# A decoder's last feed-forward layer: hidden units in seven blocks of 128 tokens in place of eight batches of 112

## The chip, the core and the metric

The kernel runs on one core of one Trainium2 chip. The metric is the device time of one execution in microseconds (us), as the median of several runs. The core has five engines with a queue each: TensorE (PE in the profile, its weight loads PEld), VectorE (DVE), ScalarE (ACT), GpSimd (POOL) and SyncE (SP), which here only issues transfers. Every queue is worked off in order, so an instruction that waits holds up all that stand behind it on its engine.

## What is computed

The reference is a decoder of four layers on `x`, 8 batches of 112 tokens with 256 features. Each layer adds an attention, a cross attention and a feed-forward part (FFN) to `x`. The change touches the last part, the FFN of layer 3, alone:

```
def nvfp4_linear(x, w, s_in):
    s_w = fp4_global_scale(w)
    xq = fake_quant_nvfp4(x, s_in)      # blocks of 16: one rounded scale, values rounded to 8 levels
    wq = fake_quant_nvfp4(w, s_w)
    return jnp.einsum('bsh,oh->bso', xq, wq)
gate_out = nvfp4_linear(x, gate_w, s_in[0])
up_out = nvfp4_linear(x, up_w, s_in[0])
hidden = jax.nn.silu(gate_out) * up_out                 # 1024 features for each token
return nvfp4_linear(hidden, down_w, s_in_down[0])
```

Its input is the normalised `x` (256 features), its result is added to `x`, and the sum is the kernel's output. Rounding acts on each token by itself, so the tokens can be cut into groups in any way.

## The kernel before

The kernel builds its program with a library that puts in the waits between engines, and that also chooses the order of instructions on each engine: among those that it takes to be ready it prefers the one that stands earlier in the program's text. Inside a `manual_schedule` block the order on PE, DVE and ACT is that of the text. A tile that is asked for under a name with one buffer (`bufs=1`) is the same memory each time, and the new use waits for the last reader of the old one.

`l3_ffn` (lines 2378 to 2485) holds the last FFN. Its weights are rounded and turned earlier (`l3_weights`, in the background of the layer 2 FFN) and lie in `self.wq`, 16 bits wide.

*Input.* The tokens come in two halves of four batches. For each half the kernel takes mean and variance of `x` (`stats`, lines 439 to 465), writes the normalised values `xn` (line 2403), their magnitudes `mag` with ACT (2410), rounds them (`quantise`), turns the rounded `xq` with eight transposes on PE (2416) and copies the turned values to `xqT` with ACT (2421). This lies outside the block with the order by hand.

*Rounding.* `quantise` is a generator: it writes instructions to DVE alone, and gives control back to its caller at each `yield`. In the order of its steps:

```
step 0   block_max: pairwise maxima of mag, 16 to 1, four instructions (L2261)
step 1   scales of the blocks, nine small instructions (L2289 to L2302)
step 2   qa = src * z                    (L2306, 32 bits)
step 3   high half | 1                   (L2309)
step 4   clip; exponent; its bound       (L2311, L2313, L2314, 16 bits)
step 5   add, subtract                   (L2316, L2317)
step 6   dst = b * scale, 1024 columns   (L2322); one more such step when n is 2048
```

*Hidden units.* `hidden(b0)` makes the 1024 hidden features of two batches, in four units of 512 columns: four matrix products on PE into `gu` (gate and up, two banks, two buffers), ACT's Silu (`sg`, 2436), DVE's product (`hid`, 2437), which frees `gu`, and ACT's magnitude (`mag`, 2440). It too is a generator, with a `yield` after each unit. Its tiles have 112 of 128 partitions in use, a token in each.

*The rounds.* The block with the order by hand runs the four units of batches 0 and 1, and then four rounds over pairs of batches. A round is `quantise` over the pair's 2 x 1024 columns, and between its steps stand: at step 2 the adds (2459) and output transfers (2460, on SP) of the pair before; at steps 2 to 5 the four units of the next pair; at steps 6 and 7 `turned` (eight transposes of one batch's rounded `hq` on PE, 2448, and one ACT copy of 896 columns into `hqT`, 2450) and `result` (eight products with the down weights into `y`, 428). In the last round `turned` of the last batch copies with DVE, and the two results and adds come after the round.

All matrix products are recorded under line 428, the helper `mm`.

Of the kernel before, what the change touches and what calls it, by code (L numbers as in the profile page):

```python
# [23 lines left out]
BF16 = mybir.dt.bfloat16  # L24
I16 = mybir.dt.int16
AF = mybir.ActivationFunctionType
ALU = mybir.AluOpType
# [4 lines left out]
P = 128  # L32
S, NB, D = 112, 8, 256
T = S * NB
HT = T // 2
HB = NB // 2
# [299 lines left out]
def drain(steps):  # L336

    while True:
        try:
            next(steps)  # L340
        except StopIteration as stop:
            return stop.value
# [31 lines left out]
class _Kernel:  # L374
# [2004 lines left out]
    def l3_ffn(self):  # L2379
        nc, tc = self.nc, self.tc  # L2380
        g, u = (m.rearrange("p (k n) -> p k n", k=2) for m in self.wq[:2])
        d = self.wq[2].rearrange("p (k n) -> p k n", k=8)
        with ExitStack() as ctx:
            acts = ctx.enter_context(tc.tile_pool(name="l3f", bufs=1))
            pool = ctx.enter_context(tc.tile_pool(name="l3f_x", bufs=1))
            work = ctx.enter_context(tc.tile_pool(name="l3f_h", bufs=2))
            ps = ctx.enter_context(tc.tile_pool(name="ps_l3f", bufs=2, space=PSUM))
            s_in, s_down = self.v("l3f_s_in"), self.v("l3f_s_in_down")

            sc = self.t(acts, [P, 3], "sc")  # L2390
            inv = self.t(acts, [P, 2], "inv")
            nc.vector.reciprocal(inv[:, 0:1], s_in)
            nc.vector.reciprocal(inv[:, 1:2], s_down)
            for i, j in enumerate((0, 0, 1)):
                nc.vector.tensor_tensor(sc[:, i : i + 1], self.igs[:, i : i + 1], inv[:, j : j + 1], ALU.mult)
            xq = self.t(acts, [P, NB, D], "xq", BF16)
            xqT = self.t(acts, [P, 2, T], "xqT", BF16)
            for half in range(2):
                b0 = half * HB
                bs = slice(b0, b0 + HB)  # L2400
                mv, rs = drain(self.stats(self.x[:, bs, :], S, HB))
                for j in range(HB):
                    nc.vector.tensor_scalar(
                        self.xn[:S, b0 + j, :].rearrange("p (e k) -> p k e", e=16),
                        self.x[:S, b0 + j, :].rearrange("p (k e) -> p k e", e=16),
                        mv[:S, j, 0:1], rs[:, j : j + 1], ALU.subtract, ALU.mult,
                    )
                flat = [a[:S, bs, :].rearrange("p b d -> p (b d)") for a in (self.xn, xq)]
                mag = self.t(pool, [P, 2, 1024], "mag")[:S, 0, :]
                nc.scalar.activation(mag, flat[0], AF.Abs)  # L2410
                for _ in self.quantise(pool, *flat, S, HB * D, D, s_in[:S], mag=mag):
                    pass
                tp = self.t(ps, [P, 2, HT], "tr16", BF16)
                for kc in range(2):
                    for j in range(HB):
                        nc.tensor.transpose(
                            tp[:, kc, j * S : (j + 1) * S],
                            xq[:S, b0 + j, kc * P : (kc + 1) * P],
                            self.ident16[:S, :S],
                        )  # L2420
                nc.scalar.copy(xqT[:, :, half * HT : (half + 1) * HT], tp)
            hids, mags, ys = {}, {}, {}

            def hidden(b0):

                hids[b0] = self.t(work, [P, 2, 1024], "hid")[:S]
                mags[b0] = self.t(pool, [P, 2, 1024], "mag")[:S]
                for j in range(2):
                    xb = self.tokens(b0 + j, xqT)
                    for i in range(2):  # L2430
                        gu = self.t(ps, [P, 2, 512], "gu")
                        cols = slice(i * 512, (i + 1) * 512)
                        for n, m in enumerate((g, u)):
                            self.mm(gu[:S, n, :], [(x, m[:, k, cols]) for k, x in enumerate(xb)])
                        sg = self.t(work, [P, 512], "sg")[:S]
                        nc.scalar.activation(sg, gu[:S, 0, :], AF.Silu, scale=sc[:S, 0:1])
                        nc.vector.scalar_tensor_tensor(
                            hids[b0][:, j, cols], gu[:S, 1, :], sc[:S, 1:2], sg, ALU.mult, ALU.mult
                        )
                        nc.scalar.activation(mags[b0][:, j, cols], hids[b0][:, j, cols], AF.Abs)  # L2440
                        yield

            hTs = {}

            def turned(b, hq, copy=nc.scalar.copy):
                tp = self.t(ps, [P, 8, S], "tr16", BF16)
                for c in range(8):
                    nc.tensor.transpose(tp[:, c, :], hq[:, c * P : (c + 1) * P], self.ident16[:S, :S])
                hTs[b] = self.t(work, [P, 8, S], "hqT", BF16)
                copy(hTs[b], tp)  # L2450

            def result(b):
                hT = hTs.pop(b)
                ys[b] = self.t(ps, [P, 512], "y")[:S, :D]
                self.mm(ys[b], [(hT[:, c, :], d[:, c, :]) for c in range(8)])

            def add(b):
                x = self.x[:S, b, :]
                nc.vector.scalar_tensor_tensor(x, ys.pop(b), sc[:S, 2:3], x, ALU.mult, ALU.add)
                nc.sync.dma_start(self.args["out"][b], x)  # L2460

            with tc.manual_schedule(engines={ET.PE, ET.DVE, ET.Activation}):
                for _ in hidden(0):
                    pass
                for b0 in range(0, NB, 2):
                    later = hidden(b0 + 2) if b0 + 2 < NB else iter(())
                    hq = self.t(work, [P, 2, 1024], "hq", BF16)[:S]
                    flat = [a.rearrange("p b d -> p (b d)") for a in (hids.pop(b0), hq)]
                    mag = mags.pop(b0).rearrange("p b d -> p (b d)")

                    for step, _ in enumerate(self.quantise(pool, *flat, S, 2048, 1024, s_down[:S], mag=mag)):
                        if step == 2 and b0 > 0:
                            add(b0 - 2)
                            add(b0 - 1)
                        if step >= 2:
                            next(later, None)
                        if step >= 6:
                            j = step - 6
                            last = b0 + j == NB - 1
                            turned(b0 + j, hq[:, j, :], nc.vector.tensor_copy if last else nc.scalar.copy)  # L2480
                            if b0 + 2 < NB:
                                result(b0 + j)
                for b in (NB - 2, NB - 1):
                    result(b)
                    add(b)
# [34 lines left out]
```

## Time and profile before

| what | us |
| --- | --- |
| median of 3 runs | 2295.76 (2290.16 to 2302.23) |
| the profiled execution, its own time | 2297.48 |
| span of its instructions | 2295.6 |
| granted TensorE clock, mean of the span | 0.952 |
| last FFN: from the add of the last cross attention result (2186.28) to the end | 109.3 |
| of it: to the first maximum of round 1 (2213.95) | 27.67 |
| the four rounds, by the first maximum of each | 18.02, 19.30, 19.30, 16.38 |
| from the last rounding step to the end | 8.65 |

Times in the views are microseconds from the start of the span. The profiled execution's own time is 1.9 us more than its span. A timeline line gives start, duration, engine, line of the code, operation, tiles and shape (partitions x elements), and in brackets how long the engine was idle before and what released it. In a table by stretch, each engine has its busy time and its number of instructions. Where two DVE instructions don't depend on each other, the next one starts up to 0.1 us before the one ahead has ended.

### The profile page before, as it was taken

Reading aid. Unit: us, or ns where it says so; the run is one execution under the profiler, and the core shown is the slowest. Engines: PE = TensorE matmul, PEld = TensorE weight load, DVE = VectorE, ACT = ScalarE, POOL = GpSimd, SP = SyncE. Lnnn points to the kernel's source line nnn. Section 1 sums busy time; section 2 is a strip of 40 time slices with the busy share of each in tenths; the row PEclk is TensorE's granted clock in tenths of the full one; section 3 lists DMA queues with packets and bytes.
Section 4 is the critical chain, followed back from the end, with each engine's and each line's share of the span. In section 5 each row is a group of like instructions: output and inputs, shape, how many; then the busy total and the mean of one; then the engine's idle time right before and its main releaser. Section 6 shows DMA issues by size and latency. Waiting matters only on the chain.

```text
span 2295.6 us, 43649 instructions
## 1 busy us (share of the span) xinstructions
PE 2095.2 (91%) x17192; PEld 1261.1 (55%) x17192; DVE 1353.8 (59%) x3894; ACT 813.3 (35%) x2336; POOL 207.5 (9%) x406
## 2 busy tenths in 40 slices
PE   6999999898998999899898988999999999799944
PEld 3444444465666566546575555566655556556623
DVE  4666666586355677643666665676710314767788
ACT  2444444461112456420232224665221011256522
POOL 0111111002012000000003422000000000100000
PEclk9999999898999999999999999999999998999956
DMA  5000001002000000011001011001200100000000
GB/s 196 3 2 2 2 21 36 31 20 101 0 1 15 19 2 20 19 34 49 1 19 38 20 64 37 2 2 38 74 37 29 44 0 1 1 1 2 2 0 16
DMA packets 9889, 57.49 MB, mean 25 GB/s; under 512 B 1114, under 2 KB 2906, under 8 KB 4698
## 3 DMA queue, kind: packets, MB, share of 16 engines
q1 hardware_dynamic: 9108, 50.01, 6.0%
q8 instruction: 137, 2.24, 0.4%
q0 software_dynamic: 432, 3.15, 0.4%
q10 hardware_dynamic: 144, 1.54, 0.2%
q14 instruction: 68, 0.56, 0.1%
HBM read 53.77 MB, written 0.92 MB: 24 GB/s over the span
## 4 chain that ended last, share of the span: by engine, by line
PE 81%; DVE 13%; ACT 3%; issue 2%; POOL 1%; DMA 0%; DVEq 0%; POOLq 0%; ACTq 0%
PE mm L428 31%; PE g L652 9%; PE gu L428 7%; PE tr L1247 6%; PE g L615 4%; PE sc L428 4%; PE mm L585 3%; PE tr L428 3%; PE av L1263 3%; PE s L428 1%; PE mm L804 1%; DVE xn L474 1%; DVE xnm L1234 1%; PE s L751 1%; PE av L428 1%
## 5 line engine op out<-in xcount | busy, mean ns | idle before, releaser
L652 PE MATMUL g<-w,hT 128*32 128x256 f32 x3552 | 236.3, 383 | 1.1 <-DVE hT L682 0.8
L1234 DVE TENSOR_REDUCE xnm<-sc 112x1 f32<-112x375 f32 x384 | 184.5, 540 | 40.8 <-PE sc L428 40.2
L1247 PEld LDWEIGHTS tr<-cst,xe 112*125 112x125 f32 x1152 | 151.4, 188 | 94.8 <-issue 37.7
L1247 PE MATMUL tr<-cst,xe 112*125 112x112 f32 x1152 | 193.0, 289 | 6.8 <-DVE xeT L1255 4.2
L428 PE MATMUL mm<-hT,w 128*128 128x448 f32 x512 | 193.0, 539 | 0.0
L652 PEld LDWEIGHTS g<-w,hT 128*32 128x32 f32 x3552 | 94.7, 109 | 107.7 <-DVE hT L682 33.1
L428 PEld LDWEIGHTS mm<-hT,w 128*128 128x128 f32 x512 | 97.1, 190 | 94.4 <-issue 94.4
L428 PE MATMUL mm<-xnT,w 128*128 128x448 f32 x316 | 134.8, 568 | 8.0 <-DVE qT L1216 2.9
L1253 ACT COPY xeT<-tr 125x336 f32<-125x336 f32 x192 | 85.4, 445 | 158.4 <-PE tr L1247 158.1
L615 PE MATMUL g<-xw,cst 128*32 128x256 f32 x1792 | 137.8, 379 | 0.0
L1255 DVE COPY xeT<-tr 125x336 f32<-125x336 f32 x192 | 97.2, 506 | 68.7 <-PE tr L1247 61.8
L428 PE MATMUL mm<-w,hT 128*112 128x256 f32 x576 | 131.2, 387 | 0.3 <-DVE x L2042 0.3
L1238 ACT ACTIVATE xe<-sc,xnm 112x375 f32<-112x375 f32 x256 | 126.6, 583 | 7.3 <-DVE xnm L1234 7.3
L428 PE MATMUL gu<-xnT,w 128*128 128x448 f32 x320 | 124.3, 543 | 1.6 <-DVE hT L1401 1.2
L428 PEld LDWEIGHTS mm<-w,hT 128*112 128x112 f32 x576 | 102.9, 181 | 26.5 <-issue 2.9
L678 ACT ACTIVATE th<-cell 128x64 f32<-128x64 f32 x224 | 57.4, 256 | 158.8 <-DVE cell L674 158.1
L2365 DVE COPY wq<-tr 128x256 bf16<-128x256 bf16 (+1 forms) x12 | 4.6, 420 | 162.7 <-PE tr L2364 162.7
L665 ACT ACTIVATE sg<-g 128x192 f32<-128x192 f32 x224 | 74.1, 331 | 73.4 <-PE g L652 63.1
L428 PEld LDWEIGHTS mm<-xnT,w 128*128 128x128 f32 x316 | 59.4, 198 | 65.7 <-issue 42.5
L428 PE MATMUL mm<-w,oT 128*112 128x256 f32 x304 | 80.3, 410 | 16.3 <-DVE oT L1875 5.3
L428 PEld LDWEIGHTS gu<-xnT,w 128*128 128x128 f32 x320 | 59.3, 190 | 61.0 <-issue 54.0
L428 PE MATMUL sc<-xkT,qT 32*112 32x375 f32 x768 | 89.8, 519 | 0.0
(451 smaller groups left out, 3647.2 us busy)
## 6 DMA issues: line engine op xcount, KB each, us to landing
w<-in_w SPq DMA_DIRECT2D x33, 1024.0 KB, 4.9
raw<-in_wq POOLq DMA_DIRECT2D x3, 1024.0 KB, 5.3
cx<-in_ctx SPq DMA_DIRECT2D x2, 1500.0 KB
w<-in_w SPq DMA_DIRECT2D x3, 896.0 KB, 4.7
wi<-in_wint SPq DMA_DIRECT2D x3, 768.0 KB, 6.0
w<-in_w SPq DMA_DIRECT2D x2, 768.0 KB, 4.1
ctxT<-in_ctxT ACTq DMA_DIRECT2D x1, 1500.0 KB, 7.9
w<-in_w SPq DMA_DIRECT2D x2, 512.0 KB, 3.5
```

The lines of the kernel that those rows point to most:

```text
L428: self.nc.tensor.matmul(out, lhsT, rhs, start=i == 0, stop=i == len(pairs) - 1)
L585: nc.tensor.matmul(pm, lhsT[k], rhs[:, k, :], start=k == 0, stop=k == 1)
L615: nc.tensor.matmul(g[32 * j : 32 * j + 32, :], pick[:, t % 16, :], xw[:, l, t // 16, 256 * j : 256 * j + 256], start=True, stop=t == 0, sk ...
L652: nc.tensor.matmul(g[32 * j : 32 * j + 32, :], hT[l][:, c, :], whh[l][:, c, 256 * j : 256 * j + 256], start=False, stop=c == 1, skip_group ...
L665: nc.scalar.activation(sg[:, :192], g[:, :192], AF.Sigmoid)
L678: nc.scalar.activation(th, cell[l], AF.Tanh)
L1234: nc.vector.tensor_reduce(nm, sc, AX.X, ALU.max, negate=True)
L1238: nc.scalar.activation(e, sc, AF.Exp, bias=nm)
L1247: nc.tensor.transpose(tp[:CH, i * S : (i + 1) * S], e[:, i * CH : (i + 1) * CH], self.ident[:S, :S])
L1253: nc.scalar.copy(eT, src)
L1255: nc.vector.tensor_copy(eT, src)
L1263: nc.tensor.matmul(avs[b][32 * j : 32 * j + 32, c * S : (c + 1) * S], values[b % 2][:CH, i, 4 * c + j, :], eTs[b, c, j][:, i, :], start=i ...
```

## The change

It does three things, all in `l3_ffn`.

1. The hidden features are made, rounded and turned for seven blocks of 128 tokens in place of eight batches of 112 (7 x 128 = 8 x 112 = 896). A block's tokens come from `xqT` by columns, across the bounds of batches. The rounds run over blocks 0-1, 2-3, 4-5 and then 6 alone. The turned blocks no longer have tiles of their own: they are columns of two arrays for all 896 tokens, `hqT[0]` (first four groups of 128 features) and `hqT[1]` (last four), which lie in the memory of `xnT` and `xn`. So a turned block takes two copies of 512 columns in place of one of 896: both on ACT, or one on DVE and one on ACT for the last block. `result` still works by batch, and reads its 112 columns from them.
2. The rounding of the input's second half is spread: its steps 0 and 1 come after the first half's turning, outside the block with the order by hand, and its steps 2 to 6 are the first thing in that block, with the four units of blocks 0 and 1 after its steps 2, 3, 4 and 5. Then its turning.
3. The statistics, normalised values and magnitudes of both halves now stand in the text ahead of the first half's rounding.

```diff
+            rounds = []
             for half in range(2):
...
                 mag = self.t(pool, [P, 2, 1024], "mag")[:S, 0, :]
                 nc.scalar.activation(mag, flat[0], AF.Abs)
-                for _ in self.quantise(pool, *flat, S, HB * D, D, s_in[:S], mag=mag):
-                    pass
+                rounds.append(self.quantise(pool, *flat, S, HB * D, D, s_in[:S], mag=mag))
+
+            def input_T(half):
                 tp = self.t(ps, [P, 2, HT], "tr16", BF16)
...
+            for _ in rounds[0]:
+                pass
+            input_T(0)
+            for _ in range(2):
+                next(rounds[1])
...
-                for j in range(2):
-                    xb = self.tokens(b0 + j, xqT)
+                for j in range(n):
+                    at = (i0 + j) * P
...
-                        for n, m in enumerate((g, u)):
-                            self.mm(gu[:S, n, :], [(x, m[:, k, cols]) for k, x in enumerate(xb)])
+                        for x, m in enumerate((g, u)):
+                            self.mm(gu[:, x, :], [(xqT[:, k, at : at + P], m[:, k, cols]) for k in range(2)])
...
-            def turned(b, hq, copy=nc.scalar.copy):
-                tp = self.t(ps, [P, 8, S], "tr16", BF16)
+            flat = self.xnT.rearrange("p k t -> p (k t)"), self.xn.rearrange("p b d -> p (b d)")[:, : 2 * T]
+            hqT = [a.bitcast(BF16).rearrange("p (c t) -> p c t", c=4) for a in flat]
+
+            def turned(i, hq, last):
+                tp = self.t(ps, [P, 8, P], "tr16", BF16)
                 for c in range(8):
-                    nc.tensor.transpose(tp[:, c, :], hq[:, c * P : (c + 1) * P], self.ident16[:S, :S])
-                hTs[b] = self.t(work, [P, 8, S], "hqT", BF16)
-                copy(hTs[b], tp)
+                    nc.tensor.transpose(tp[:, c, :], hq[:, c * P : (c + 1) * P], self.ident16)
+                cols = slice(i * P, (i + 1) * P)
+                (nc.vector.tensor_copy if last else nc.scalar.copy)(hqT[0][:, :, cols], tp[:, :4, :])
+                nc.scalar.copy(hqT[1][:, :, cols], tp[:, 4:, :])
 
             def result(b):
-                hT = hTs.pop(b)
                 ys[b] = self.t(ps, [P, 512], "y")[:S, :D]
-                self.mm(ys[b], [(hT[:, c, :], d[:, c, :]) for c in range(8)])
+                self.mm(ys[b], [(hqT[c // 4][:, c % 4, b * S : (b + 1) * S], d[:, c, :]) for c in range(8)])
...
-                for _ in hidden(0):
-                    pass
-                for b0 in range(0, NB, 2):
-                    later = hidden(b0 + 2) if b0 + 2 < NB else iter(())
...
+                later = hidden(0, 2)
+                for step, _ in enumerate(rounds[1]):
+                    if step < 4:
+                        next(later)
+                input_T(1)
+
+                for i0 in range(0, 7, 2):
+                    n = 1 if i0 == 6 else 2
+                    later = hidden(i0 + 2, min(2, 5 - i0)) if n == 2 else iter(())
...
+                    for step, _ in enumerate(self.quantise(pool, *flat, P, n * 1024, 1024, s_down, mag=mag)):
+                        if step == 2 and i0 > 0:
+                            add(i0 - 2)
+                            add(i0 - 1)
                         if step >= 2:
                             next(later, None)
                         if step >= 6:
                             j = step - 6
-                            last = b0 + j == NB - 1
-                            turned(b0 + j, hq[:, j, :], nc.vector.tensor_copy if last else nc.scalar.copy)
-                            if b0 + 2 < NB:
-                                result(b0 + j)
+                            turned(i0 + j, hq[:, j, :], n == 1)
+                            if n == 2:
+                                result(i0 + j)
```

More of the change, by code (lines that the diff above doesn't have):

```diff
@@ L2417, in l3_ffn @@
                             tp[:, kc, j * S : (j + 1) * S],
-                            xq[:S, b0 + j, kc * P : (kc + 1) * P],
+                            xq[:S, half * HB + j, kc * P : (kc + 1) * P],
                             self.ident16[:S, :S],
@@ L2421, in l3_ffn, with hidden @@
                 nc.scalar.copy(xqT[:, :, half * HT : (half + 1) * HT], tp)
-            hids, mags, ys = {}, {}, {}
-            def hidden(b0):
-                hids[b0] = self.t(work, [P, 2, 1024], "hid")[:S]
-                mags[b0] = self.t(pool, [P, 2, 1024], "mag")[:S]
-                for j in range(2):
-                    xb = self.tokens(b0 + j, xqT)
+            for _ in rounds[0]:
[3 more added lines that the diff above has]
+                next(rounds[1])
+            hids, mags, ys = {}, {}, {}
+            def hidden(i0, n):
+                hids[i0] = self.t(work, [P, 2, 1024], "hid")[:, :n, :]
+                mags[i0] = self.t(pool, [P, 2, 1024], "mag")[:, :n, :]
+                for j in range(n):
+                    at = (i0 + j) * P
                     for i in range(2):
@@ L2432, in hidden @@
                         cols = slice(i * 512, (i + 1) * 512)
-                        for n, m in enumerate((g, u)):
-                            self.mm(gu[:S, n, :], [(x, m[:, k, cols]) for k, x in enumerate(xb)])
-                        sg = self.t(work, [P, 512], "sg")[:S]
-                        nc.scalar.activation(sg, gu[:S, 0, :], AF.Silu, scale=sc[:S, 0:1])
+                        for x, m in enumerate((g, u)):
+                            self.mm(gu[:, x, :], [(xqT[:, k, at : at + P], m[:, k, cols]) for k in range(2)])
@@ L2437, in hidden @@
+                        sg = self.t(work, [P, 512], "sg")
+                        nc.scalar.activation(sg, gu[:, 0, :], AF.Silu, scale=sc[:, 0:1])
                         nc.vector.scalar_tensor_tensor(
-                            hids[b0][:, j, cols], gu[:S, 1, :], sc[:S, 1:2], sg, ALU.mult, ALU.mult
+                            hids[i0][:, j, cols], gu[:, 1, :], sc[:, 1:2], sg, ALU.mult, ALU.mult
                         )
-                        nc.scalar.activation(mags[b0][:, j, cols], hids[b0][:, j, cols], AF.Abs)
+                        nc.scalar.activation(mags[i0][:, j, cols], hids[i0][:, j, cols], AF.Abs)
@@ L2441, in hidden @@
                         yield
-            hTs = {}
-            def turned(b, hq, copy=nc.scalar.copy):
-                tp = self.t(ps, [P, 8, S], "tr16", BF16)
+            flat = self.xnT.rearrange("p k t -> p (k t)"), self.xn.rearrange("p b d -> p (b d)")[:, : 2 * T]
+            hqT = [a.bitcast(BF16).rearrange("p (c t) -> p c t", c=4) for a in flat]
+            def turned(i, hq, last):
+                tp = self.t(ps, [P, 8, P], "tr16", BF16)
                 for c in range(8):
-                    nc.tensor.transpose(tp[:, c, :], hq[:, c * P : (c + 1) * P], self.ident16[:S, :S])
-                hTs[b] = self.t(work, [P, 8, S], "hqT", BF16)
-                copy(hTs[b], tp)
+                    nc.tensor.transpose(tp[:, c, :], hq[:, c * P : (c + 1) * P], self.ident16)
+                cols = slice(i * P, (i + 1) * P)
+                (nc.vector.tensor_copy if last else nc.scalar.copy)(hqT[0][:, :, cols], tp[:, :4, :])
+                nc.scalar.copy(hqT[1][:, :, cols], tp[:, 4:, :])
@@ L2462, in l3_ffn @@
             with tc.manual_schedule(engines={ET.PE, ET.DVE, ET.Activation}):
-                for _ in hidden(0):
-                    pass
-                for b0 in range(0, NB, 2):
-                    later = hidden(b0 + 2) if b0 + 2 < NB else iter(())
[L2467 to L2474, printed above, removed]
+                later = hidden(0, 2)
[6 more added lines that the diff above has]
+                    later = hidden(i0 + 2, min(2, 5 - i0)) if n == 2 else iter(())
+                    hq = self.t(work, [P, 2, 1024], "hq", BF16)[:, :n, :]
+                    flat = [a.rearrange("p b d -> p (b d)") for a in (hids.pop(i0), hq)]
+                    mag = mags.pop(i0).rearrange("p b d -> p (b d)")
+                    for step, _ in enumerate(self.quantise(pool, *flat, P, n * 1024, 1024, s_down, mag=mag)):
+                        if step == 2 and i0 > 0:
+                            add(i0 - 2)
+                            add(i0 - 1)
                         if step >= 2:
```

## The prediction, made before the changed kernel was run

> **What bounds the kernel now.** I read the page's slices first, to see whether the changed part has one limit or several.
>
> ```profile
> span 2295.6 us, 43649 instructions
> ...
> PE   6999999898998999899898988999999999799944
> ...
> DVE  4666666586355677643666665676710314767788
> ```
>
> PE is full nearly everywhere, but a slice is 57 us, and in the last two (from about 2181) PE drops to 4 tenths and DVE rises to 8. So the last FFN is another kind of stage, and a change there is worth what DVE saves, not PE. Next the busy time of each engine in seven stretches, cut at DVE's marks: end of the first half's rounding, first maximum of rounds one to four, last rounding step. Columns: stretch, length, busy time (instructions) of PE, PEld, DVE, ACT, POOL, then granted clock, DMA share, GB/s.
>
> ```profile
> 2186.28:2198.83 12.55, 0.00 (x0) 0.00 (x0) 12.38 (x43) 2.11 (x2) 0.00 (x0) 0.64 0.00 0
> 2198.83:2213.95 15.12, 10.42 (x38) 5.53 (x39) 10.27 (x21) 7.96 (x12) 0.00 (x0) 0.61 0.00 0
> 2213.95:2231.97 18.02, 5.41 (x17) 2.31 (x16) 17.33 (x26) 4.79 (x8) 0.00 (x0) 0.50 0.00 0
> 2231.97:2251.27 19.30, 10.47 (x52) 7.28 (x50) 18.21 (x29) 6.75 (x10) 0.00 (x0) 0.68 0.05 13
> 2251.27:2270.57 19.30, 10.96 (x52) 7.48 (x50) 18.21 (x30) 6.75 (x10) 0.00 (x0) 0.68 0.04 12
> 2270.57:2286.95 16.38, 5.65 (x36) 4.69 (x34) 15.73 (x25) 1.81 (x2) 0.00 (x0) 0.50 0.05 14
> 2286.95:2295.60 8.65, 4.80 (x29) 4.15 (x26) 1.60 (x4) 0.91 (x1) 0.00 (x0) 0.68 0.10 28
> ```
>
> DVE is busy 94 to 96% of every round: the rounds are its work. Only the second stretch has slack (10.27 of 15.12). DVE's timeline there names it:
>
> ```profile
> 2207.37 0.75 DVE L2437 SCALAR_TENSOR_TENSOR hid<-gu,sc,sg 112x512 f32<-112x512 f32 x1
> 2210.48 0.75 DVE L2437 SCALAR_TENSOR_TENSOR hid<-gu,sc,sg 112x512 f32<-112x512 f32 x1 [2.36 <-ACT sg L2436]
> 2212.51 0.75 DVE L2437 SCALAR_TENSOR_TENSOR hid<-gu,sc,sg 112x512 f32<-112x512 f32 x1 [1.27 <-ACT sg L2436]
> 2213.95 1.23 DVE L2261 TENSOR_TENSOR qm<-mag 112x1024 f32<-112x1024 f32 x1 [0.70 <-ACT mag L2440]
> ```
>
> The second half's rounding is over at 2207.4, two units of the first pair are left, and DVE waits 2.36 + 1.27 + 0.70 = 4.33 us on ACT.
>
> **Does a DVE instruction cost more on 128 partitions than on 112?** The sum hangs on it: 7 x 128 tokens are as many elements as 8 x 112. The rounding of the weights ran the same line with 128 partitions (min/median/max in ns):
>
> ```profile
> L2306 DVE TENSOR_TENSOR qa<-raw,qz x6: 1215/1226/1226, 1619.4 to 1859.2; 128x1024 f32<-128x1024 f32 x6
> L2306 DVE TENSOR_TENSOR qa<-hid,qz x4: 2291/2291/2292, 2220.1 to 2276.7; 112x2048 f32<-112x2048 f32 x4
> L2306 DVE TENSOR_TENSOR qa<-xn,qz x2: 1207/1216/1226, 2192.3 to 2201.4; 112x1024 f32<-112x1024 f32 x2
> ```
>
> 1226 against 1216: the columns set the time. The other rounding lines agree (L2309 693 against 688, L2316 692 against 688). So a block costs what a batch did, and there is one less. The first row also prices the lone block: 1024 columns take 53% of 2048, not half.
>
> **Step A, up to round one.** The chain from the first half's last rounding step (2198.83) to the first Silu's end (2202.80 + 0.69) took 4.66: transposes 0.93, copy 0.91, four products at half clock, Silu. This doesn't change. What may move is its start. Half two's small statistics and normalised values now stand earlier in the text, so its magnitudes come earlier, and some of its steps 0 and 1 may slip between the first half's rounding steps. I take three small instructions at 0.1 net, 0.3 in all: first `hid` at 2203.8. From there each `hid` waits for the Silu behind the magnitude of the one before: 2.03 from start to start (2210.48 to 2212.51). The rounding steps between them (0.69; 0.43 three times; 0.69 twice, each beside a `hid` of 0.66 net) take up to 2.05, so they fit this pace. Three intervals, 6.09, then 1.44 from the last `hid` to the maximum (2212.51 to 2213.95): round one starts at 2211.3, **2.65 earlier**. Bounds: at best all of DVE's 4.33 goes. At worst the 2.55 of small instructions that followed the first half's last rounding step (2198.83 to 2201.37) all slip ahead of it; then round one starts at 2213.6 and gains 0.35. I take the middle, since the trace shows two such chains alternating (2187 to 2198), not one running ahead. Queued behind a waiting `hid` are only the rounding steps of the second half, which round one needs anyway; its turning (PE, ACT) has 8 us until a unit of round one is wanted. Two new waits cost nothing: both halves share one `mag`, but the first maximum frees it at 2188.1, and the second half's values come at 2192 or later; and the turned blocks lie in `xn` and `xnT`, whose last reader is `qa` of the second half, some 25 us before the first copy.
>
> **Step B, rounds one to three.** Round one keeps its 18.02. In round two the first unit waited 0.41 on PE, which had worked through transposes, copy, `y` twice, 3.70 apart (2252.73 to 2256.43). Now: transposes 0.93 x 128/112 = 1.06 at most (+0.13); first copy of 512 columns 0.59 in place of 0.91 (ACT rows: 896 columns 0.906, 512 from PSUM 0.586 and 0.597; -0.32); the first four products read only that copy, and take 1.0, longer than the second copy. So -0.19 a block, -0.35 a round: 18.95. Bounds: if `y` waited for both copies, 0.51 more, so +0.32 a block. Round three has two units in place of four: 16.38 (the round without units) + 2 x 0.66 + waits of 0.05 and 0.14 = 17.9, **1.4 less**.
>
> **Step C, the lone block.** Maxima 0.72 + 0.46 + 0.32 + 0.25 = 1.75, scales on 64 columns 2.55 (2198.83 to 2201.37), `qa` 1.26: at 5.55 the adds of the third pair stand in DVE's queue. One takes 0.43, at 5.98; the second needs the pair's last `y`. In the round before they were covered:
>
> ```profile
> 2270.57 1.22 DVE L2261 TENSOR_TENSOR qm<-mag 112x1024 f32<-112x1024 f32 x1
> ...
> 2275.72 1.96 PE L428 MATMUL y<-wq,hqT 128*112 128x256 bf16 x8 [0.99 <-ACT hqT L2450]
> ...
> 2276.72 2.29 DVE L2306 TENSOR_TENSOR qa<-hid,qz 112x2048 f32<-112x2048 f32 x1
> ```
>
> `y` ended 7.11 after the round's start, and `qa` at 8.44. With half the columns the cover is gone: by step B `y` ends at 6.75, so DVE **waits 0.8**, a wait that was not there. Then the add 0.45 and the last six rounding steps, 4.25 with the destination: 11.45 in place of 16.38, **4.93 less**. The output transfers go with their adds; SP has nothing else.
>
> **Step D, the tail.** Before, the first of two turned batches was ready 2.03 after its rounding step, and the last rounding step stood 0.6 behind it. Now the lone block follows it: 1.06 + a DVE copy of 512 columns, 0.42 (rows: 256 columns 0.288, 896 0.623, 1024 0.685) + handovers 0.2 = 1.7, then 16 products, add and transfer as before (2288.39 to 2295.60, 7.21): 8.9 in place of 8.65, **0.25 more**. ACT's copy of the other half (0.59) lies beside the first four products (0.92). Before, the last copies of ACT (2287.43) and DVE (2288.20) read two tiles; now both read one bank. The Trainium skill (PSUM — Partial Sum Buffer, PSUM bank collisions raise a hardware error) says that two engines must not read one bank at once, even at disjoint columns, so one copy would have to follow the other. No row here shows that; DVE's first costs nothing (2.4 against 2.6 when the fifth product is due), ACT's first 0.6.
>
> **Sum.** -2.65 - 0.35 - 1.4 - 4.93 + 0.25 = -9.1. The span goes from 2295.6 to 2286.5, the profiled execution's 2297.48 to 2288.4. That execution stands 1.7 above the median of the runs shown; on the median, 2295.76 - 9.1 = **2286.7**, 0.40% less. 0.5%, 11.5 us, is about what a measurement of this kernel can tell from no change; the forecast lies 2.4 us inside it.
>
> **Rivals.**
> 1. *More is won at the start.* All of DVE's 4.33 goes (+1.7) and the lone round's wait too (+0.8): -11.6, 2284.2. For it: DVE has rounding work enough. Against it: the 2.03 pace is ACT's, and the work between fills it only just. Chance 0.15.
> 2. *The start stays late and `y` waits for both copies.* +2.3 at the start; 0.51 a block, so 1.0 in each of three places (rounds two and three, the lone round's wait), 3.0: -3.8, 2292.0. For it: outside the block by hand the order is the library's. Against it: the products name their half of the features. Chance 0.15.
> 3. *Slower: time goes with partitions.* If an instruction on 128 took 128/112 of its time on 112, the rounds (adds apart) would be 20.6, 21.6, 20.3 and 12.3, the units' pace 2.32, so round one would start at 2212.4, and the end come at 2212.4 + 74.8 + 9.0 = 2296.2, 0.6 slower: 2296.4. It decides from 14% per instruction on; the row above shows 0.8%, so chance 0.05, most of it below what can be told.
>
> **How the numbers follow.** The forecast has 0.65. Its terms can be off by 2 us and the three runs shown lie 12 us apart, so about four in ten of it would measure beyond 11.5, with most of rival 1 and little of rival 2: faster 0.42, within 0.5% 0.54, slower 0.04. The range takes in rivals 1 and 2 and some 4 us of a median's own spread on the low side, 2 on the high: 2280 to 2293.
>
> **What would show it.** Right: 14 `hid` in place of 16, with unchanged 0.75; the first maximum over a block near 25 us after the last cross attention add, with `hid` every 2.03 before it; rounds of 18.0, 18.95, 17.9, 11.45; `x` (L2459) waiting 0.8 on `y` in the last; ACT copies of 0.59. Wrong: `hid` or `qa` longer than 0.75 and 2.29; the first `hid` after 2206; ACT's second copy as the releaser of `y`; anything before 2186 in another place.

## The result, and the profile after

| what | before | after |
| --- | --- | --- |
| median of 19 runs each, us | 2294.87 (2287.93 to 2302.23) | 2285.55 (2276.80 to 2290.39) |
| the profiled execution, its own time | 2297.48 | 2277.92 |
| span of its instructions | 2295.6 | 2275.7 |
| last cross attention add | 2186.28 | 2175.91 |
| last FFN, from that add to the end | 109.32 | 99.79 |

The ratio of the times is 0.9956, with a 95% interval of 0.9944 to 0.9968: 0.44% faster, 10.1 us (7.3 to 12.9) of 2294.87; the medians lie 9.3 us apart. The forecast was 9.1 us. The spans of the two profiled executions lie 19.9 us apart, twice as much, so they must not be subtracted as wholes. The page of after shows the slices as they were:

```profile
span 2275.7 us, 43609 instructions
...
DVE  4666666686355677642766666676720314657778
```

The last two slices are still DVE's. To see where the time went, the last FFN of after is cut at the marks that the prediction used for before. Columns as there: stretch, length, busy time (instructions) of PE, PEld, DVE, ACT, POOL, granted clock, DMA share, GB/s.

```profile
2175.91:2188.86 12.95, 0.00 (x0) 0.00 (x0) 12.78 (x45) 2.11 (x2) 0.00 (x0) 0.63 0.00 0
2188.86:2201.09 12.23, 6.98 (x24) 2.76 (x26) 9.53 (x19) 7.12 (x10) 0.00 (x0) 0.64 0.00 0
2201.09:2219.12 18.03, 8.32 (x29) 3.31 (x30) 17.34 (x26) 5.84 (x9) 0.00 (x0) 0.59 0.00 0
2219.12:2237.93 18.81, 9.55 (x50) 5.71 (x49) 18.12 (x30) 7.08 (x12) 0.00 (x0) 0.68 0.05 14
2237.93:2255.74 17.81, 8.94 (x42) 5.96 (x41) 17.05 (x28) 4.67 (x8) 0.00 (x0) 0.60 0.05 13
2255.74:2267.10 11.36, 5.33 (x30) 4.31 (x27) 10.00 (x24) 2.15 (x4) 0.00 (x0) 0.50 0.07 20
2267.10:2275.70 8.60, 4.43 (x24) 3.92 (x24) 1.39 (x3) 0.59 (x1) 0.00 (x0) 0.70 0.09 27
```

The second mark lies 0.08 ahead of the end of the first half's last rounding step (2188.94); cut there, the first two stretches are 13.03 and 12.15. Read it against before: the first two stretches together went from 27.67 to 25.18 and their DVE work from 22.65 to 22.31, so 2.15 of the 2.49 won there is slack. The last round went from 16.38 to 11.36, and the other rounds changed by 0.01, -0.49 and -1.49. The start and the lone round are 7.5 of the 9.5 won. DVE's timeline between the first `hid` and round one:

```profile
2193.57 0.75 DVE L2445 SCALAR_TENSOR_TENSOR hid<-gu,sc,sg 128x512 f32<-128x512 f32 x1 [1.61 <-ACT sg L2444]
...
2195.60 0.75 DVE L2445 SCALAR_TENSOR_TENSOR hid<-gu,sc,sg 128x512 f32<-128x512 f32 x1 [0.67 <-ACT sg L2444]
...
2201.09 1.23 DVE L2261 TENSOR_TENSOR qm<-mag 128x1024 f32<-128x1024 f32 x1
```

Three waits of 2.36, 1.27 and 0.70, before the third and fourth `hid` and the first maximum, have become two of 1.61 and 0.67, before the first and second `hid`. The other two units and the first maximum follow without a wait. In round two the first unit waited for its Silu, and now it does not (first before, then after):

```profile
2241.61 0.75 DVE L2437 SCALAR_TENSOR_TENSOR hid<-gu,sc,sg 112x512 f32<-112x512 f32 x1 [0.40 <-ACT sg L2436]
```

```profile
2228.27 0.74 DVE L2445 SCALAR_TENSOR_TENSOR hid<-gu,sc,sg 128x512 f32<-128x512 f32 x1
```

The lone round of after, with PE's second `y` between:

```profile
2260.13 1.23 DVE L2306 TENSOR_TENSOR qa<-hid,qz 128x1024 f32<-128x1024 f32 x1
...
2261.36 1.06 PE L428 MATMUL y<-wq,xn 128*112 128x256 bf16 x4
...
2262.45 0.48 DVE L2469 SCALAR_TENSOR_TENSOR x<-y,sc,x 112x256 f32<-112x256 f32 x1 [0.71 <-PE y L428]
```

`y` ends at 2262.42, 6.68 after the round's start; `qa` was over at 2261.36. This is the new wait that step C named.

### The profile page after: what moved, and what is told of

The parts are those of the page before. It is cut to its first block, busy times and chain, and to the rows that moved or that the text cites. A ratio compares the mean times of both kernels' runs of the same rounds, so it can differ in the third digit from the quotient of the medians.

```text
span 2275.7 us, 43609 instructions
## 1 busy us (share of the span) xinstructions
PE 2080.1 (91%) x17173; PEld 1250.8 (55%) x17176; DVE 1346.9 (59%) x3891; ACT 810.5 (36%) x2338; POOL 206.9 (9%) x406
## 4 chain that ended last, share of the span: by engine, by line
PE 80%; DVE 14%; ACT 2%; issue 2%; POOL 1%; DMA 0%; DVEq 0%; POOLq 0%; ACTq 0%
PE mm L428 31%; PE g L652 9%; PE gu L428 7%; PE tr L1247 6%; PE g L615 4%; PE sc L428 4%; PE mm L585 3%; PE av L1263 3%; PE tr L428 3%; PE s L428 1%; PE mm L804 1%; DVE xn L474 1%; DVE xnm L1234 1%; PE av L428 1%; PE s L751 1%
```

## The experiments

Each row of the table is one profiled execution. Since whole executions scatter (last section), a kernel is judged by the stage, from the last cross attention add to the end, and by its parts: to round one, rounds one to four, tail. Only the last two were also timed. "The changed kernel" is the one after the change, with 25.18, 18.03, 18.81, 17.81, 11.36, 8.60.

| kernel | to round one | one | two | three | four | tail | stage |
| --- | --- | --- | --- | --- | --- | --- | --- |
| before | 27.67 | 18.02 | 19.30 | 19.30 | 16.38 | 8.65 | 109.32 |
| after | 25.18 | 18.03 | 18.81 | 17.81 | 11.36 | 8.60 | 99.79 |
| e1_blocks_only | 27.68 | 18.02 | 18.88 | 17.81 | 11.37 | 8.81 | 102.57 |
| e2_spread_only | 25.25 | 18.04 | 19.13 | 19.30 | 16.40 | 8.61 | 106.73 |
| e3_adds_later | 25.20 | 18.02 | 18.88 | 17.81 | 10.63 | 8.89 | 99.43 |
| e4_copies_swapped | 25.19 | 18.02 | 18.81 | 18.79 | 11.47 | 9.41 | 101.69 |
| e5_hand_order | 25.19 | 18.04 | 18.86 | 17.81 | 11.36 | 8.71 | 99.97 |
| e6_abs_behind | 24.74 | 17.80 | 18.65 | 17.86 | 11.37 | 8.83 | 99.25 |
| e7_two_banks | 25.20 | 18.04 | 18.88 | 17.81 | 11.36 | 8.33 | 99.62 |
| e8_three_moves | 24.73 | 17.80 | 18.64 | 17.51 | 10.64 | 7.77 | 97.09 |
| e9_three_moves_hand | 24.29 | 17.80 | 18.65 | 17.50 | 10.57 | 8.06 | 96.87 |

**Each half of the change alone.** The blocks without the spread rounding: the changed kernel, with the input part of before.

```diff
-            for _ in rounds[0]:
-                pass
-            input_T(0)
-            for _ in range(2):
-                next(rounds[1])
...
-                later = hidden(0, 2)
-                for step, _ in enumerate(rounds[1]):
-                    if step < 4:
-                        next(later)
-                input_T(1)
+                for _ in hidden(0, 2):
+                    pass
```

> Seven blocks as in the changed kernel, but the input is rounded as before: each half to its end, one after the other, and the four units of blocks 0 and 1 behind it. Measure: length of the last FFN, from the last add of the cross attention to the end of the span (109.3 before, 99.8 changed), and in it the time to the first maximum of round one (27.7 before, 25.2 changed). Theory (the spread of the second half's rounding gives the start's gain, the blocks give the rest): 27.7 to round one, then the changed kernel's rounds 18.0, 18.8, 17.8, 11.4 and tail 8.6: 102.3 in all. Rival (the start gains from the blocks, not from the spread): 25.2 and 99.8.

And the spread rounding without the blocks: before, with those lines the other way round.

> Eight batches of 112 as before, but the second half's input rounding is spread among the first four units as in the changed kernel. Theory (start and blocks add up): 25.2 to round one, then the old rounds 18.0, 19.3, 19.3, 16.4 and tail 8.65: 106.8. Rival (the spread does nothing by itself, DVE's waits come back in the first round): 109.3, with round one longer than 18.0.

Measured: the blocks alone take 102.57, 6.75 less than before, with the start of before to within 0.01 (27.68; waits of 2.37, 1.27 and 0.70). The spread alone takes 106.73, 2.59 less: 25.25 to round one, and the rounds those of before but for 0.17 in round two. 6.75 + 2.59 = 9.34 of the 9.53: the two halves add, and they touch different waits. The earlier statistics (part 3 of the change) go with the spread rounding in both kernels, so what they do alone is not shown. The whole execution of the second was 2298.92 us, 6.3 above before's run beside it, though its last FFN was shorter: its add came at 2190.47, 4.2 later than in the profile of before, in code that no kernel here changes.

**The wait in the lone round.** The adds of the third pair stand one rounding step later:

```diff
-                        if step == 2 and i0 > 0:
+                        if step == (3 if n == 1 else 2) and i0 > 0:
```

> The changed kernel, with the third pair's two adds one rounding step later in the lone block's round (behind L2309, 0.72). Theory (DVE's wait of 0.71 for the pair's last product stands on the path that sets the end): wait gone, lone round 10.7, length 99.1. Rival (the wait is hidden, since the lone block's transposes or the results wait for PE anyway): lone round shorter, but the tail longer by as much, length 99.8.

Measured: the lone round takes 10.63, 0.73 less, and the wait of 0.71 is gone. A high half of 0.69 now fills it:

```profile
2264.83 0.69 DVE L2309 TENSOR_SCALAR qb<-qa 128x1024 int16<-128x1024 int16 x1
2265.44 0.94 DVE L2469 SCALAR_TENSOR_TENSOR x<-y,sc,x 112x256 f32<-112x256 f32 x2
```

The stage is only 0.36 shorter, 99.43 for the 99.1 expected, since the tail took 8.89 in place of 8.60. That is not the wait come back, as the rival has it: from the last rounding step to the first add it is 3.61, as in after (3.60), but the last four products ran at half clock, 1.06 in place of 0.79. So step C's wait cost its whole length.

**The order of the two copies.** ACT's copy of the last four groups first, in all blocks; the products still read the first four groups first.

```diff
+                nc.scalar.copy(hqT[1][:, :, cols], tp[:, 4:, :])
                 (nc.vector.tensor_copy if last else nc.scalar.copy)(hqT[0][:, :, cols], tp[:, :4, :])
-                nc.scalar.copy(hqT[1][:, :, cols], tp[:, 4:, :])
```

> The changed kernel, with the two copies of a turned block in the other order, so that the first product needs the second copy: its cost bounds what starting on the first copy is worth. Theory: each y starts 0.49 later in rounds one to three, which rounds two and three hide (the first Silu now has over 1 us to spare), but the lone round's wait does not: 0.71 becomes 1.2; for the last block ACT's copy comes first, DVE's follows it because both read one bank, and y starts 0.6 later: length 99.8 + 0.5 + 0.6 = 100.9. Rival (one bank may be read by both engines at once, or products wait for both copies in any case): tail unchanged, length 99.8 to 100.3.

Measured: the stage takes 101.69, 1.9 more, and 0.8 more than expected. In the tail DVE's copy now waits for ACT's:

```profile
2284.54 0.42 DVE L2461 COPY xnT<-tr 128x512 bf16<-128x512 bf16 x1 [1.74 <-ACT xn L2460]
```

From the transposes to the first `y` it is 2.17 in place of 1.55, the 0.6 of the prediction. In the rounds a block's chain is 3.97 from first `y` to second in place of 3.49. Round two hides that and round three, against the expectation, does not: there the first unit waits 0.95, the delay of two blocks. Round three of after had nothing to spare (its first Silu ends at 2247.10, the adds at 2247.16). What hides it in round two is the clock: the second `y` of round two ran at full clock (0.65 for four products), that of round three at half (1.10). The lone round's wait was 0.81, again with its second `y` at full clock. So the price that rival 2 puts on "`y` waits for both copies" is real where the order makes it so, some 0.5 a block, but only where the clock doesn't cover it.

**What holds the start.** The two waits that are left, 1.61 and 0.67, could be a lack of DVE work at that place (the order of the library) or the chain of PE and ACT. First, the first half's rounding, its turning and the second half's steps 0 and 1 moved into the order by hand:

```diff
-            for _ in rounds[0]:
-                pass
-            input_T(0)
-            for _ in range(2):
-                next(rounds[1])
...
             with tc.manual_schedule(engines={ET.PE, ET.DVE, ET.Activation}):
+                for _ in rounds[0]:
+                    pass
+                input_T(0)
+                for _ in range(2):
+                    next(rounds[1])
                 later = hidden(0, 2)
```

> The changed kernel, with the first half's rounding and turning and the second half's steps 0 and 1 put into the order by hand, so that nothing of the second half's steps stands between the first half's. Measure: time from the last cross attention add to the first unit's hid (17.66 changed) and to round one (25.18). Theory (the first unit's wait of 1.61 is there because eight small instructions of the second half slip ahead of the first half's last rounding step, but they run there beside others at little cost): the first half is turned about 1.0 earlier, and what slipped ahead is paid behind it without overlap, so hid moves by 0.3 at most: 24.9 to 25.2, length 99.5 to 99.9. Rival (the chain from the first half's turning sets the first unit): hid 1.0 earlier, 24.2, length 98.8.

Measured: the first half's rounding ends 0.8 earlier (12.23 after the add in place of 13.03), there is no wait before the first `hid`, and it is 25.19 to round one: nothing won.

```profile
2199.71 0.75 DVE L2440 SCALAR_TENSOR_TENSOR hid<-gu,sc,sg 128x512 f32<-128x512 f32 x1
...
2201.73 0.75 DVE L2440 SCALAR_TENSOR_TENSOR hid<-gu,sc,sg 128x512 f32<-128x512 f32 x1 [0.67 <-ACT sg L2439]
```

The first `hid` stands where it stood (17.7 after the add), and the units' loop of 2.03 (`hid` 0.75, its magnitude 0.63, the next Silu 0.67) takes the rest. Second, that loop made shorter: ACT's magnitude goes behind the next unit's Silu, which DVE is waiting for.

```diff
                         nc.scalar.activation(sg, gu[:, 0, :], AF.Silu, scale=sc[:, 0:1])
+                        if pend:
+                            nc.scalar.activation(*pend.pop(), AF.Abs)
...
-                        nc.scalar.activation(mags[i0][:, j, cols], hids[i0][:, j, cols], AF.Abs)
+                        pend.append((mags[i0][:, j, cols], hids[i0][:, j, cols]))
+                        if j == n - 1 and i == 1:
+                            nc.scalar.activation(*pend.pop(), AF.Abs)
```

> The changed kernel, with ACT's magnitude of a unit issued behind the Silu of the next unit in place of ahead of it (the last of a group follows its unit). Theory (the 2.03 between two hid at the start is the loop hid, magnitude, Silu on ACT): the loop is cut, the second unit's wait of 0.67 goes, round one starts 0.7 earlier (24.5), and in the rounds the waits of about 0.14 before a second unit go, 0.4 in all: length 98.7. Rival (DVE's own work or the products on PE set the 2.03): 25.2, length 99.8.

Measured: 24.74 to round one, 0.44 less, and rounds one and two 0.2 less each. The second wait falls from 0.67 to 0.35, not to nothing: the second Silu now waits 1.02 for PE's `gu`, whose products go at half clock here (granted clock 0.50 from 2199.6 to 2204.0).

```profile
2202.82 0.69 ACT L2444 ACTIVATE sg<-gu,sc 128x512 f32<-128x512 f32 x1 [1.02 <-PE gu L428]
2203.54 0.75 DVE L2447 SCALAR_TENSOR_TENSOR hid<-gu,sc,sg 128x512 f32<-128x512 f32 x1 [0.35 <-ACT sg L2444]
```

So 0.44 came of the expected 0.7, and the rest stops at the next engine. In round three the first unit waits 0.26, which it did not in after. From the end of the second `y` to the first Silu it is 2.08, against 1.80 in e7_two_banks. The clock is not the cause: it was 0.50 in both, and PE's products stand at the same distances. But the Silu starts 0.38 after the end of its unit's fourth product, where it is 0.10 in e7_two_banks. It is 0.38 in e8_three_moves too, at full clock, so this 0.28 goes with the move; why is open.

**Two banks for the last block.** The eight transposes of the lone block go to two tiles of one bank each, four to a tile.

```diff
-                tp = self.t(ps, [P, 8, P], "tr16", BF16)
+                tps = [self.t(ps, [P, 8, P], "tr16", BF16) for _ in range(2 if last else 1)]
                 for c in range(8):
+                    tp = tps[c // 4 if last else 0]
```

> The changed kernel, with the last block's eight transposes in two tiles of one bank each in place of one, so that DVE's copy can start after four transposes and beside ACT's. Theory (in the tail the two copies read one bank one after the other, and the first waits for all eight transposes): y starts 0.5 earlier, tail 8.3 to 8.4 at half clock, length 99.3. Rival (the products then wait for ACT's copy, which needs the last transpose and 0.59): y's fifth product is late, tail 8.6 to 8.9.

Measured: the tail takes 8.33, against 8.81 to 8.89 of the kernels whose last products also ran at half clock: 0.5 less. First the last copies of after, then those of this kernel:

```profile
2268.23 0.42 DVE L2460 COPY xnT<-tr 128x512 bf16<-128x512 bf16 x1 [1.13 <-PE tr L2458]
2268.69 0.59 ACT L2461 COPY xn<-tr 128x512 bf16<-128x512 bf16 x1 [7.79 <-DVE xnT L2460]
```

```profile
2277.78 0.42 DVE L2461 COPY xnT<-tr 128x512 bf16<-128x512 bf16 x1 [0.70 <-PE tr L2460]
2278.20 0.59 ACT L2462 COPY xn<-tr 128x512 bf16<-128x512 bf16 x1 [7.33 <-PE tr L2460]
```

In after DVE waits 1.13, for all eight transposes, and ACT is released by DVE's copy. Here DVE waits 0.70, for four, and ACT is released by PE. The gain is DVE's earlier start: ACT's copy was hidden behind the first four products in both. The two copies did not come to run at one time even here (DVE ends at 2278.20, where ACT starts), so what a true overlap would give is not shown.

**The three together.** The adds later, the magnitude behind, the two banks.

> The changed kernel with the three moves that each shortened the last FFN by itself: the adds one rounding step later in the lone round (-0.73), ACT's magnitude behind the next Silu (-0.44 before round one, -0.4 in rounds one and two), the last block's turned values in two banks (-0.5). Theory (the three waits lie one behind the other on DVE's path, so the gains add): from the last cross attention add to the end 98.0 us, against 99.8 (100.05 with the last products at half clock) after the change: to round one 24.7, rounds 17.8, 18.65, 17.85, 10.65, tail 8.35. In the timed runs some 11.3 us under before, ratio 0.995. Rival (the gains share one cover: an earlier round two or three uncovers PE's chain of turning and y): each is won once, but 0.3 to 1.0 comes back as a wait of the first unit of round two or three, and the stage is 98.3 to 99.

And with the start in the order by hand as well:

> As e8_three_moves, with the first half's rounding, its turning and steps 0 and 1 of the second half's rounding also in the order by hand, so that the first hid has no wait. By itself that move gained nothing, since DVE's work was only put elsewhere and the units' loop (2.0 us each, Silu and magnitude) took up the rest. Theory (that loop is now shorter, so DVE's own work is what is left): round one starts 0.2 to 0.4 earlier than in e8_three_moves, 24.3 to 24.5, and the stage takes 97.6 to 97.8. Rival (the loop is now held by the products at half clock on PE): round one at 24.7 as in e8_three_moves, 98.0.

Measured: 97.09 and 96.87. The gains of the first two moves are there in the first (24.73, 10.64), and DVE's copy waits 0.70 as in e7_two_banks. No wait came back in round three, but its second `y` ran at full clock; whether the 0.26 would have come back at half clock, as the rival has it, is not shown. The sum of 98.0 was passed by 0.9, which is clock: round three 17.51 for 17.85, where its two Silu now run back to back, and the tail 7.77 for 8.35, with the last two groups of four products in 0.85 and 0.60 in place of 1.06. In the second, round one starts at 24.29, as its theory said: what gained nothing alone is worth 0.44 once the loop behind it is shorter.

```profile
2203.42 0.75 DVE L2442 SCALAR_TENSOR_TENSOR hid<-gu,sc,sg 128x512 f32<-128x512 f32 x1
...
2204.68 0.74 DVE L2442 SCALAR_TENSOR_TENSOR hid<-gu,sc,sg 128x512 f32<-128x512 f32 x1
```

There are no brackets left here: neither `hid` waits, and 23.2 of the 24.29 are DVE busy. Timed, the ratios to before are 0.9948 (0.9927 to 0.9968) and 0.9952 (0.9933 to 0.9970). Both beat before, and by the stage both beat after, by 2.7 and 2.9 us, of which some 0.9 is the clock of one execution. That is 0.12% of the whole, and the intervals of the times can't tell them from after's 0.9956.

## Why the prediction was right

- **What bounds it.** DVE's work in the rounds and its waits on ACT in the start. Right: the rounds moved by the instructions and the waits that left DVE's queue, and taking a wait away moved the part that it stood in by about as much or more (0.71 gone: -0.73; 0.32: -0.44; 0.43: -0.5). The exception is e5_hand_order, where the wait of 1.61 went and nothing was won: other work had taken its place.
- **Partitions.** The columns set a DVE instruction's time, not its partitions. Right, and rival 3 is out:

```profile
L2306 DVE TENSOR_TENSOR qa<-hid,qz x4: 1226/2293/2294, 2207.3 to 2260.1; 128x2048 f32<-128x2048 f32 x3, 128x1024 f32<-128x1024 f32 x1
```

  2293 for 2048 columns on 128 partitions, where 112 took 2291; `hid` 750 against 748 (medians). The Trainium skill (VectorE: DVE Perf Modes, Why `tensor_reduce` can't reduce along partition axis) says that each of the 128 lanes is a pipeline of its own; these rows agree.
- **Step A**, -2.65: measured -2.49 (2.50 are lost when the spread alone is undone, 2.42 won with the spread alone). The first `hid` came at 17.66 after the add, for 17.5 in the forecast, since the first half's rounding ended 0.48 later than before (13.03 for 12.55) in place of 0.3, with two more of half two's small instructions ahead of its last step; the chain from there took 4.63 for 4.66. From the first `hid` to round one it is 7.52 for 7.53, with the four `hid` 2.03, 2.02 and 2.03 apart. DVE waits in the first of these intervals alone; the others are filled by its work, as worked out.
- **Step B**, -0.35 in round two and -1.4 in round three: measured -0.49 and -1.49. In the four kernels with this change alone there (e1, e3, e5, e7) whose second `y` ran at half clock, as in before, round two took 18.86 to 18.88, -0.42 to -0.44; the first unit's wait of 0.40 is about all that was there to win. The two `y` of a pair stand 3.49 apart for 3.70 before, -0.21 for the -0.19 worked out. (The wait and the times that the prediction gives there are those of round three; round two of before has 0.40 and 3.69, so its sum stands.) The price of the second copy was the right one to ask about, as the swapped copies showed.
- **Step C**, -4.93 with a wait of 0.8: measured -5.02 with 0.71. `y` ended at 6.68 for 6.75.
- **Step D**, +0.25: measured -0.05, the one term with a wrong sign. The chain was right: 1.61 from the last rounding step to the first `y` for 1.7, and the kernels whose last products ran at half clock to the end (e1, e3, e6) show 8.81 to 8.89 for 8.9. After itself had its last four in 0.79 in place of 1.06, and e5_hand_order in 0.89. So the sign is the clock's, which the prediction could not know. The bank was read by one engine after the other, DVE first, as assumed: ACT starts 0.04 after DVE's copy ends. By the Trainium skill (PSUM — Partial Sum Buffer, PSUM bank collisions raise a hardware error) they must not overlap there; the trace shows that the program keeps them apart, with DVE's copy as ACT's releaser, and not what the chip would do.
- **The sum**, -9.1: the stage shows -9.53, the medians of 19 runs -9.3. Of the 0.4 that the stage won beyond the forecast, 0.3 is step D's and so luck. Nothing before the last FFN need have changed, though the last cross attention add came 10.4 us earlier in after's profile. The prediction named that ("anything before 2186 in another place") as a sign that it would be wrong. It is no such sign: among the nine executions of the experiments, where this part is unchanged too, the add comes between 2179.3 and 2190.5, with 11.2 us between e3_adds_later and e4_copies_swapped, whose text ahead of it is the same.
- **Rivals.** Rival 1 (all of DVE's waits go) did not happen in the change. In e9_three_moves_hand DVE has no wait left at the start or in the lone round, but the start gained 3.38, not rival 1's 4.33, since DVE is busy for 23.2 there in place of 22.65, and its small gaps without a wait come to 1.1 in place of 0.7. This kernel is 12.45 under before, for the 11.6 that rival 1 gave, by moves that rival 1 does not name. Rival 2 did not happen: the start did not stay late, and the products read their own half of the features (PE waits 0.68 for ACT's first copy, where it waited 0.99 to 1.00 for the whole one).

## What to carry to other kernels

Where an engine's work fills a stage, count its instructions and their columns: rows of tokens packed from 112 to 128 partitions cost DVE nothing and save whole instructions. A shorter round loses its covers, so for each wait that it had hidden ask what then ends last, and move the waiting instruction behind work that needs no waiting. When one move gains nothing because the next limit stands right behind it, try the two together before dropping it; and compare stages, not whole executions, where a change is worth less than their scatter.

## What the runs showed of the hardware that was not expected

**The same code at two clocks.** The last cross attention add lies up to 14.6 us apart between executions (2175.9 to 2190.5). For before and after, some 7 of the 10.4 us arise in one place, in code that is the same. Busy time by engine from 420 to 430, first before, then after, with the granted clock third from the end:

```profile
420.00:430.00 10.00, 9.93 (x29) 4.66 (x29) 3.11 (x5) 4.00 (x9) 0.00 (x0) 0.50 0.00 0
```

```profile
420.00:430.00 10.00, 9.32 (x54) 4.86 (x55) 4.63 (x10) 7.56 (x30) 0.00 (x0) 1.00 0.00 0
```

PE is busy throughout in both, but in before at half clock, 29 matrix instructions for 54. In stretches of 2 us the low clock lasts from about 418.5 to 432.2, with PE busy 97% or more of each from 420 on; by our estimate 13.7 us at half clock are 6.8 us of lost work, which is the size of the shift. The episode is not of one execution alone: the granted clock over these 10 us is 0.50 in the profiles of e2, e4 and e6 too, and 1.00 in the other seven. The Trainium skill (TensorE: Matmul & The Clock Gate, Part 1: The HAM clock gate) has the full clock return after some 3.4 us of sustained work; here it took four times as long. Why is open.

**Weights of 128 columns load faster than of 112.** The first products' loads went from 184 ns (128x112, mean of 64) to 130 ns (128x128, mean of 56), though they are larger; loads for `y`, still of 112 columns, took 196 to 210. It is not the clock: in one stretch of after at half clock (2241.2 to 2245.6) the loads of 112 columns took 202 and 212, those of 128 columns for the first products 147. The Trainium skill (TensorE: Matmul & The Clock Gate, Weight-path perf modes — Fast Weight Load (FWL) and DoubleRow) says that the fast load is on with 128 weights in a type other than fp32; these rows agree. Nothing here waited for it: the loads lie beside products.
